# The last recurrent step of a gated graph network computed with nodes on partitions instead of features

## The chip, the cores and the metric

The kernel runs on one core of one Trainium2 chip. The metric is the device time of one execution in microseconds (us). Engines are named as the profile names them: PE is TensorE (matmuls and transposes; PEld is its loading of the stationary operand), DVE is VectorE, ACT is ScalarE, POOL is GpSimd, SP is SyncE, which starts DMAs. [...]

## The reference, cut to what matters

There are 64 graphs of 256 nodes with 256 features each, and two layers. Layer 0 normalizes the nodes' features, takes the positive part and then does three steps of a gated recurrent unit over the graph, whose result is added to x. Layer 1 normalizes again, does graph attention with four heads, and adds that to x.

```
h = relu(layernorm(x))
for i in range(3):                                 # layer 0
    m = h @ weight[i]
    aggr = A^T m                                   # A = (adj != 0)
    r = sigmoid(aggr W_ir^T + b_ir + h W_hr^T + b_hr)
    z = sigmoid(aggr W_iz^T + b_iz + h W_hz^T + b_hz)
    n = tanh(aggr W_in^T + b_in + r * (h W_hn^T + b_hn))
    h = (1 - z) * n + z * h
x = x + h
h = relu(layernorm(x))                             # layer 1
x = x + attention(h, adj, W, b, a)
```

## The kernel before, in words

Two graphs make a pair (PB = 2), so there are 32 pairs of T = 512 nodes. All of the network is done for a pair, and the pairs follow one another in an order that is written out by hand: `at(tick, phase, p, fn)` files a function under a tick, a phase (STEP, then READY, then REST) and a pair, and at the end all are emitted tick by tick, within a phase the later pair first. Nothing reorders them afterwards.

One recurrent step is an object of class `Step`, and it takes six ticks, `tick_0` to `tick_5`. In the steady state three slots of six ticks follow each other: the third step of pair p (slot A in the prediction), the second step of pair p+1 (slot B), the first step of pair p+2 (slot C). In a slot's ticks stands, besides, layer 1 of earlier pairs: its matmuls `po` (L542), its divisions on DVE (L551, L553), its additions to x on POOL (L558), the masks' maxima `any` on DVE (L899), leaky (L919) and exponentials on ACT.

The state is kept transposed in `hT`: features on partitions, two blocks of 128 (KD = 2), nodes in the free dimension. Gates are computed in the same layout. A `block` (L308) is one gate's product for one graph of the pair, or for a sum of both graphs' operands: four fp32 matmuls, the weights stationary (128x128), 256 nodes moving, into one PSUM bank of 512 columns. The products are shared out so that seven instead of eight are needed for a square of products; so there are sums and differences (T1 to T4, T2n, T3n, T4n) on DVE and partial results that are added in PSUM. A `part` (L417) is one matmul of 128x256 of the state's own share of n; there are seven, named N00, N01, NS1 to NS4 and N11.

In `tick_0`, the aggregation (`pa`) multiplies the state with nodes on partitions, split in two halves hNhi and hNlo, with the edges. So at the end of each step the state has to be turned: `back(l, i)` (ticks 7 and 8 of the step, phase REST) does four PE transposes (L770) for each graph into a bank `pback`, and for the first two steps writes hNhi on ACT (L760) and hNlo on DVE (L761). After the third step `residual` (L776) adds the turned state to x on DVE instead.

The steps that the prediction speaks of:

- `tick_1`: NS2 into bank `qb`; DVE's addition (L453) of the first half of `qb` and `m5n` into the second half; the block into `pc`; the part N01.
- `tick_2`: the parts NS3 (it reads T3n, L418) and NS4 into the two halves of `qb`; S1's block. NS3 writes the half that L453 read, and so has to wait for it.
- `state_n` (L421, ACT): the state's share of n is copied out of PSUM with its bias.
- `tanh_half` (L425, ACT): two instructions of 128x256 for R or Z, as each feature block has its own bias per partition.
- `first_n` (L495, DVE): (R+1) * hn into the bank `pn`; `input_n` adds a block onto it; `new_n` (L506 ACT, L510 POOL): two tanhs of 128x256 give n, and POOL subtracts it from the state.
- `update(i)` (L527, L528, DVE): R = (Z+1) * R, then hT = R/2 + n; both graphs' updates stand in phase READY of the tick after `tick_5`, the first tick of the next slot.

PSUM has five banks for gates (`gate_bank`) and three for all else (`bank`). The last pair has a sequence of its own, `plan_tail`, in which layer 1 of the two last pairs is interleaved.

Of the kernel before, what the change touches and what calls it, by code (L numbers as in the profile page):

```python
# [26 lines left out]
def gated_gnn_then_gat_kernel(  # L27
# [69 lines left out]
    def bank(name):  # L97
# [3 lines left out]
        "x": 5, "adj": 2, "edge": 2, "noedge": 2, "hT_a": 2, "xn": 2, "val": 2, "row": 4, "zz": 4, "o": 2,  # L101
# [44 lines left out]
    w_msgs += [load_square("row", f"w_msg_{l}", weight[l]) for l in range(1, L)]  # L146
# [39 lines left out]
    bhn = const.tile([P, KD], F32, name="bhn")  # L186

# [120 lines left out]
    def block(pt, w, j, src, start=False):  # L308

        for c in range(KD):  # L310
            for k in range(KD):
                nc.tensor.matmul(  # L312
                    pt[:, ts(c, N)], w[:, k, j * D + c * P : j * D + (c + 1) * P], src[:, k, :],
                    start=start and c == 0 and k == 0, stop=(c == KD - 1 and k == KD - 1),
                    skip_group_check=True,
                )

# [66 lines left out]
    class Step:  # L384


        def __init__(self, n_, l, hT, end):

            self.n_, self.l, self.hT, self.end = n_, l, hT, end
# [25 lines left out]


# [5 lines left out]

        def tanh_half(self, i, dst, src, g0):
            for c in range(KD):
                nc.scalar.activation(  # L425
                    of(dst, i)[:, c, :], src[:, c, :], AF.Tanh, bias=brz[:, g0 + c : g0 + c + 1], scale=0.5
                )

        def tick_0(self, hN, edge):
            h0 = of(self.hT(), 0)  # L430
            q_a, q_b = self.bank("qa"), self.bank("qb")
            self.part(q_a[:, :N], N00, h0[:, 0, :], start=True)
            nc.scalar.copy(q_b[:, :N], q_a[:, :N])
            aggr = self.own("aggr", [P, KD, T])
            for e in range(KD):
                pt = bank(f"pa_{self.n_}_{e}")
                for i in range(PB):
                    for s in range(KN):
                        for half in range(2):
                            nc.tensor.matmul(  # L440
                                pt[:, ts(i, N)], hN[half][:, i * KN + s, ts(e, P)], edge[:, i * KN + s, :],
                                start=(s == 0 and half == 0), stop=(s == KN - 1 and half == 1),
                            )
                nc.scalar.copy(aggr[:, e, :], pt)
            self.part(q_a[:, N:], NS1, self.T1[:, 0, :])
            nc.scalar.copy(self.own("m5n", [P, N]), q_a[:, N:])  # L446

        def tick_1(self):
            h0 = of(self.hT(), 0)
            q_a, q_b = self.qa, self.qb  # L450
            self.own("hn", [P, KD, T])
            self.part(q_b[:, :N], NS2, self.T2n)
            nc.vector.tensor_add(q_b[:, N:], q_b[:, :N], self.m5n)  # L453
            p_c = self.bank("pc")
            block(p_c, w_h, RH, h0, start=True)
            self.part(q_a[:, :N], N01, h0[:, 1, :])
            self.state_n(0, 0, q_a[:, :N])
            self.bank("p5")
            nc.scalar.copy(self.bank("pd"), p_c)
            T3 = self.own("T3", [P, KD, N])  # L460
            nc.vector.tensor_sub(T3, of(self.aggr, 1), of(self.hT(), 1))
            nc.vector.tensor_add(self.own("T2", [P, KD, N]), T3, h0)

        def tick_2(self):
            q_b = self.qb
            self.part(q_b[:, :N], NS3, self.T3n)
            self.part(q_b[:, N:], NS4, of(self.hT(), 1)[:, 1, :])
            nc.vector.scalar_tensor_tensor(
                of(self.hn, 1)[:, 1, :], q_b[:, :N], bhn[:, 1:2], self.m5n, op0=ALU.add, op1=ALU.add
            )  # L470
            self.state_n(0, 1, q_b[:, N:])
            block(self.p5, w_a[self.l], S1, self.T1, start=True)
            nc.scalar.copy(self.own("m5", [P, T]), self.p5)
            nc.vector.tensor_sub(self.own("T4", [P, KD, N]), self.T2, of(self.aggr, 0))

        def tick_3(self):
            R_ = self.own("R", [P, KD, T])
            block(self.pd, w_a[self.l], S2, self.T2)
            nc.vector.tensor_add(self.bank("pe"), self.pd, self.m5)
            block(self.pc, w_a[self.l], RA, of(self.aggr, 0))  # L480
            self.tanh_half(0, R_, by_c(self.pc), 0)

        def tick_4(self):
            Z_ = self.own("Z", [P, KD, T])
# [3 lines left out]
            block(self.pd, w_h, RZ, self.T3)  # L488
            nc.vector.tensor_add(of(Z_, 1), by_c(self.pd), by_c(self.m5))
            block(self.pe, w_a[self.l], S4, of(self.aggr, 1))  # L490
# [8 lines left out]
        def input_n(self, i):  # L499
            block(getattr(self, f"pn{i}"), w_a[self.l], NA, of(self.aggr, i))  # L500

        def new_n(self, i):
# [6 lines left out]
            if not (self.end and i == 1):  # L509
                nc.gpsimd.tensor_sub(of(self.R, i), of(self.hT(), i), n__)  # L510

        def tick_5(self):
# [3 lines left out]
            block(self.pd, w_a[self.l], ZA, self.T4)  # L516
# [5 lines left out]
        def update(self, i):  # L522

            d_ = of(self.R, i)
            if self.end and i == 1:
                nc.vector.tensor_sub(d_, of(self.hT(), i), of(self.hn, i))
            nc.vector.scalar_tensor_tensor(d_, of(self.Z, i), 1.0, d_, op0=ALU.add, op1=ALU.mult)  # L527
            nc.vector.scalar_tensor_tensor(of(self.hT(), i), d_, 0.5, of(self.hn, i), op0=ALU.mult, op1=ALU.add)  # L528

# [33 lines left out]
    def plan_tail(t0, p, v, g, turn_back, residual):  # L563


        val, zz, own, drow, mrow = None, {}, {}, {}, {}
# [22 lines left out]
        def result(i):  # L589
            if i == 0:  # L590
# [99 lines left out]
        def do(what, q, *key):  # L690
# [3 lines left out]
        order = (  # L694
            lambda: g.update(0), do("rows", 1), do("product", 2, 0), lambda: turn_back(0), lambda: g.update(1),
            do("product", 2, 1), lambda: residual(0), lambda: stats(0), do("add", 1), lambda: turn_back(1),
            do("product", 2, 2), lambda: residual(1), lambda: result(0), lambda: turned(0), lambda: stats(1),
            do("product", 2, 3), do("divided", 2, 0), lambda: values(0), lambda: result(1), lambda: turned(1),
            do("divided", 2, 1), do("divided", 2, 2), lambda: values_out(0), do("divided", 2, 3),
            do("write", 2), lambda: spread_scores(0), lambda: logits(0), lambda: leaky(0),  # L700
            lambda: values(1), lambda: values_out(1), lambda: maxima(0), do("exps", 1, 0), lambda: spread_scores(1),
            lambda: logits(1), lambda: leaky(1), lambda: spread_tops(0), do("product", 1, 0), do("product", 1, 1),
            lambda: maxima(1), lambda: spread_tops(1), do("exps", 1, 1), do("divided", 1, 0), do("divided", 1, 1),
            lambda: exps(0), do("product", 1, 2), do("product", 1, 3), lambda: exps(1), do("divided", 1, 2),
            do("divided", 1, 3), do("write", 1), lambda: output(0), lambda: output(1),
        )
        for k, fn in enumerate(order):
            at(t0 + SUB * (2 * L - 1) + 0.01 * (k + 1), READY, p, fn)

    def plan_pair(p):  # L710
# [40 lines left out]
        def back(l, i):  # L751

            def fn():
                if l < L - 1 and i == 0:
                    v["hN"] = node_halves(f"{p}_{l}")
                turn_back(l, i)
                pt = v["pback", i]
                hi, lo = (flat(y[:, i * KN : (i + 1) * KN, :]) for y in v["hN"])
                if l < L - 1:
                    nc.scalar.copy(hi, pt)  # L760
                    nc.vector.tensor_sub(lo, pt, hi)  # L761
                else:
                    residual(i)
            return fn

        def turn_back(l, i):
            pt = v["pback", i] = bank(f"pback_{p}_{l}_{i}")
            for s in range(KN):
                for k in range(KD):
                    nc.tensor.transpose(  # L770
                        pt[:, s * D + k * P : s * D + (k + 1) * P], h["hT"][:, k, ts(i * KN + s, P)], ident
                    )

        def residual(i):
            xi = flat(v["x"][:, i * KN : (i + 1) * KN, :])
            nc.vector.tensor_add(xi, v["pback", i], xi)  # L776

        for l in range(L):
            end = last and l == L - 1
            g = Step(f"{p}_{l}", l, lambda: h["hT"], end)  # L780
            t = 2 * SUB * l
            ready(t - 3 if l else t - 1, g.state_sums)
            ready(t + 2, g.last_state_sum)
            step(t, lambda g=g: g.tick_0(v["hN"], v["edge"]))
            for k, fn in enumerate((g.tick_1, g.tick_2, g.tick_3, g.tick_4, g.tick_5), 1):
                step(t + k, fn)
            if not end:
                ready(t + SUB, lambda g=g: g.update(0))
                ready(t + SUB, lambda g=g: g.update(1))
                for i in range(PB):  # L790
# [16 lines left out]
        if last:  # L807
            plan_tail(t0, p, v, g, lambda i: turn_back(L - 1, i), residual)
# [169 lines left out]
    at(2, REST, 0, load_vectors)  # L978
    at(5, REST, 0, lambda: step_weights_T(1))
# [38 lines left out]
```

## Time and profile before

| | |
|---|---|
| Median of 3 runs | 2533.7 us (2533.55 to 2534.89) |
| Profiled execution, its own time | 2540.86 us |
| Its span in the profile | 2539.1 us, mean PE clock 0.995 |
| PE busy | 2514.5 us, 99% of the span |
| DVE busy | 1824.1 us, 72% |
| ACT busy | 1466.2 us, 58% |
| POOL busy | 645.5 us, 25% |
| PE transposes of the state (L770) | 768, busy 116.1 us |

The profile shows one execution; its durations are read from it, and the median is what times are compared with. Busy times of matmuls overlap, as they are pipelined, so a PE operation is priced by the distance from its start to the start of the next. An "idle" figure in a row is the time that the engine stood still just before it, and the name behind the arrow is what it waited for.

### The profile page before, as it was taken

How to read it: one execution, taken by the hardware profiler on the slowest of the kernel's cores; microseconds unless marked ns; L12 is line 12 of the kernel's file. 1: busy time of each engine (PE TensorE's matmuls, PEld its weight loads, DVE VectorE, ACT ScalarE, POOL GpSimd, SP SyncE). 2: the span in 40 equal slices, each digit the busy share in tenths (PEclk: the TensorE clock that was granted, in tenths of full speed). 3: DMA queues.
4: the chain of work that ended last, by engine and by line, in shares of the span. 5: the costliest groups of instructions: out<-in, count | busy, mean ns of one | idle time of the engine just before them, and what ended most of it. 6: DMA issues, size and time to landing. Idle time of an engine off the chain costs nothing.

```text
span 2539.1 us, 38539 instructions
## 1 busy us (share of the span) xinstructions
PE 2514.5 (99%) x13918; PEld 2246.4 (88%) x13918; DVE 1824.1 (72%) x4458; ACT 1466.2 (58%) x3095; POOL 645.5 (25%) x514
## 2 busy tenths in 40 slices
PE   8999999999999999999999999999999999999998
PEld 6888898888889888989888988888988889898887
DVE  5567777677777777776777776777777777767667
ACT  3456565565555565555665655655656656556664
POOL 0122232222222222323232323222222223222221
PEclk9999999999999999999999999999999999999998
DMA  3033434553435544345544444534344544354443
GB/s 94 17 74 88 97 93 108 109 125 92 92 92 117 109 113 99 87 95 117 117 100 93 98 102 109 125 92 100 88 113 109 119 95 93 87 124 110 93 95 89
DMA packets 168223, 251.91 MB, mean 99 GB/s; under 512 B 42896, under 2 KB 128352, under 8 KB 168032
## 3 DMA queue, kind: packets, MB, share of 16 engines
q0 software_dynamic: 33728, 130.03, 26.6%
q1 hardware_dynamic: 132736, 119.41, 16.0%
q8 instruction: 110, 1.80, 0.3%
q14 instruction: 81, 0.66, 0.1%
q10 hardware_dynamic: 1568, 0.01, 0.0%
HBM read 215.62 MB, written 25.67 MB: 95 GB/s over the span
## 4 chain that ended last, share of the span: by engine, by line
PE 97%; DVE 1%; DMA 1%; ACT 1%; issue 0%; POOL 0%; SPq 0%; DVEq 0%
PE pd L312 20%; PE pn L312 13%; PE pc L312 13%; PE po L542 9%; PE pa L440 7%; PE qb L418 6%; PE pe L312 6%; PE p L312 6%; PE qa L418 5%; PE pv L820 4%; PE pback L770 3%; PE pt_a L370 1%; PE pt_b L370 1%; PE pc L238 1%; DVE any L899 0%; DMA hh_nat<-in_L_gnn_w_hh_dram 0%
## 5 line engine op out<-in xcount | busy, mean ns | idle before, releaser
L510 POOL TENSOR_TENSOR R<-hT_a,hn 128x512 f32<-128x512 f32 x191 | 317.8, 1664 | 879.4 <-ACT hn L506 821.5
L312 PE MATMUL pn<-aggr,w_a 128*128 128x256 f32 x1536 | 367.1, 382 | 0.0
L312 PE MATMUL pd<-T,w_a 128*128 128x256 f32 x1536 | 366.3, 381 | 0.0
L312 PEld LDWEIGHTS pn<-aggr,w_a 128*128 128x128 f32 x1536 | 287.0, 190 | 43.1 <-DVE pn L495 6.4
L312 PEld LDWEIGHTS pd<-T,w_a 128*128 128x128 f32 x1536 | 287.9, 191 | 37.6
L542 PEld LDWEIGHTS po<-val,zz 128*128 128x128 f32 x2048 | 250.3, 195 | 4.5
L542 PE MATMUL po<-val,zz 128*128 128x65 f32 x2048 | 247.2, 275 | 0.0
L899 DVE CUSTOM_DVE_ANT_0 any<-drow,noedge 128x256 f32<-128x256 f32 x496 | 236.9, 478 | 9.8 <-DMA drow<-score_dram 1.0
L506 ACT ACTIVATE hn<-pn,bi 128x256 f32<-128x256 f32 x384 | 160.3, 469 | 144.3 <-PE pn L312 144.2
L425 ACT ACTIVATE R<-pc,brz 128x256 f32<-128x256 f32 x192 | 80.5, 470 | 278.5 <-PE pc L312 278.5
L527 DVE SCALAR_TENSOR_TENSOR R<-Z,R 128x512 f32<-128x512 f32 x192 | 131.8, 687 | 147.6 <-POOL R L510 142.8
L558 POOL TENSOR_TENSOR x<-x,o 128x256 f32<-128x256 f32 x124 | 112.0, 904 | 481.6 <-DVE o L553 481.6
L761 DVE TENSOR_TENSOR hNlo<-pback,hNhi 128x512 fp32r<-128x512 f32 x128 | 88.4, 691 | 201.6 <-ACT hNhi L760 201.6
L919 ACT ACTIVATE zz<-zz,val 128x256 f32<-128x256 f32 x496 | 224.9, 509 | 0.0
L495 DVE SCALAR_TENSOR_TENSOR pn<-R,hn 128x512 f32<-128x512 f32 x192 | 142.5, 742 | 93.7 <-ACT hn L421 77.2
L425 ACT ACTIVATE R<-pe,brz 128x256 f32<-128x256 f32 x192 | 80.5, 470 | 185.9 <-PE pe L312 185.9
L528 DVE SCALAR_TENSOR_TENSOR hT_a<-R,hn 128x512 f32<-128x512 f32 x192 | 174.6, 909 | 14.3 <-ACT m5n L446 1.4
L312 PE MATMUL pd<-T,w_h 128*128 128x256 f32 x768 | 181.5, 379 | 0.0
L312 PE MATMUL pc<-aggr,w_a 128*128 128x256 f32 x768 | 181.5, 379 | 0.0
L312 PE MATMUL pe<-aggr,w_a 128*128 128x256 f32 x768 | 181.4, 379 | 0.0
L312 PE MATMUL pc<-hT_a,w_h 128*128 128x256 f32 x768 | 181.4, 379 | 0.0
L312 PE MATMUL p<-T,w_a 128*128 128x256 f32 x768 | 181.4, 379 | 0.0
(176 smaller groups left out, 5258.5 us busy)
## 6 DMA issues: line engine op xcount, KB each, us to landing
zz<-score_dram POOLq DMA_DIRECT2D x62, 1024.0 KB, 11.7
zz<-topT_dram POOLq DMA_DIRECT2D x62, 1024.0 KB, 8.7
adj<-in_adj_dram SPq DMA_DIRECT2D x64, 512.0 KB
drow<-score_dram SPq DMA_DIRECT2D x62, 512.0 KB
x<-in_x_dram SPq DMA_DIRECT2D x32, 512.0 KB
out_dram<-x SPq DMA_DIRECT2D x31, 512.0 KB
noedge_dram<-noedge SPq DMA_DIRECT2D x31, 256.0 KB
score_dram<-score SPq DMA_DIRECT2D x124, 4.0 KB
```

Of the source, the lines that this page charges most:

```text
L312: nc.tensor.matmul(pt[:, ts(c, N)], w[:, k, j * D + c * P : j * D + (c + 1) * P], src[:, k, :], start=start and c == 0 and k == 0, stop=(c ...
L418: nc.tensor.matmul(pt, w_n[:, j, :], src, start=start, stop=True, skip_group_check=True)
L425: nc.scalar.activation(of(dst, i)[:, c, :], src[:, c, :], AF.Tanh, bias=brz[:, g0 + c : g0 + c + 1], scale=0.5)
L440: nc.tensor.matmul(pt[:, ts(i, N)], hN[half][:, i * KN + s, ts(e, P)], edge[:, i * KN + s, :], start=(s == 0 and half == 0), stop=(s == KN ...
L495: nc.vector.scalar_tensor_tensor(by_c(self.bank(f"pn{i}")), of(self.R, i), 1.0, of(self.hn, i), op0=ALU.add, op1=ALU.mult)
L506: nc.scalar.activation(n__[:, c, :], p_n[:, c, :], AF.Tanh, bias=bi[:, 2 * KD + c : 2 * KD + c + 1])
L510: nc.gpsimd.tensor_sub(of(self.R, i), of(self.hT(), i), n__)
L527: nc.vector.scalar_tensor_tensor(d_, of(self.Z, i), 1.0, d_, op0=ALU.add, op1=ALU.mult)
L528: nc.vector.scalar_tensor_tensor(of(self.hT(), i), d_, 0.5, of(self.hn, i), op0=ALU.mult, op1=ALU.add)
L542: nc.tensor.matmul(po[:, ts(h_, VC)], zz[:, j, h_, ts(s, P)], v["val"][:, i * KN + j, ts(h_, VC)], start=(j == 0), stop=(j == KN - 1),)
L899: nc.vector.tensor_tensor_reduce(any_, drow[r // KN][:, h, :], v["noedge"][:, r, :], 1.0, -3.0e38, ALU.add, ALU.max, accum_out=v["top"][:, ...
L919: nc.scalar.activation(zz[:, h, :], zz[:, h, :], AF.Prelu, alpha=ALPHA, bias=v["val"][:, r, S0 + H + h : S0 + H + h + 1],)
```

## The change

The third step of layer 0 gets a class of its own, `LastStep`, in which nodes are on partitions and features in the free dimension. Its `block` has the state stationary and the weights moving, with as many matmuls of the same size; each `part` becomes two matmuls of 128x128. The result comes out as x is stored, so the third step has no `back` and no `residual`; its update adds to x directly, in three DVE operations for each graph: x += n, R = (Z+1) * R, x += R/2. For that, the state before the step is needed with nodes on partitions in full precision: `back` of the second step copies it to a buffer `h` on ACT.

Biases now run along the free dimension, so they can't be given to ACT as one value per partition. Four rows, broadcast to all partitions (`b_rows`), are loaded with six DMAs at tick 3 and combined by four DVE operations at tick 9. R's bias is put into the bank `pc` by an ACT copy at tick 0 (`seed`), n's into both `pn` banks by ACT copies in tick 4; Z's is added by DVE in tick 4, and that of the state's share of n by DVE in `state_n` and `last_state_n`. `state_n` of this step moves from ACT to DVE. The tanhs become one instruction of 512 in place of two of 256. `first_n` writes to SBUF, and `new_n` adds it to the bank on DVE before the tanh.

The order changes too. In tick 5, `pn0` and `pn1` come before ZA's block; `new_n(1)` and Z's tanh of graph 0 move to phase REST of tick 5; the update moves from phase READY of the next tick to its phase REST. In the tail graph 1 comes first. The buffers tagged `row` go from 4 to 2, and two of the weights are loaded into buffers tagged `noedge`. Here is the diff's core.

```diff
-        "x": 5, "adj": 2, "edge": 2, "noedge": 2, "hT_a": 2, "xn": 2, "val": 2, "row": 4, "zz": 4, "o": 2,
+        "x": 5, "adj": 2, "edge": 2, "noedge": 2, "hT_a": 2, "xn": 2, "val": 2, "row": 2, "zz": 4, "o": 2,
...
+    class LastStep(Step):
+        both = [P, PB, KN * D]
+        def mine(self, y, i):
+            return by_c(y[:, i, :])
+        def block(self, pt, w, j, src, start=False):
+            for s in range(KN):
+                for k in range(KD):
+                    nc.tensor.matmul(
+                        pt[:, ts(s, D)], src[:, k, ts(s, P)], w[:, k, ts(j, D)],
+                        start=start and s == 0 and k == 0, stop=(s == KN - 1 and k == KD - 1),
+                        skip_group_check=True,
+                    )
+        def part(self, pt, j, src, start=False):
+            for s in range(KN):
+                nc.tensor.matmul(
+                    pt[:, ts(s, P)], src[:, ts(s, P)], w_n[:, j, :], start=start and s == 0, stop=True,
+                    skip_group_check=True,
+                )
...
+        def state_n(self, c, i, pt):
+            nc.vector.tensor_add(
+                self.mine(self.hn, i)[:, :, ts(c, P)], pt.rearrange("q (s n) -> q s n", s=KN), self.row(BH, c)
+            )
+        def tanh_half(self, i, dst, src, g0):
+            nc.scalar.activation(self.mine(dst, i), src, AF.Tanh, scale=0.5)
+        def first_term(self):
+            return self.pc, False
+        def seed(self):
+            nc.scalar.copy(by_c(self.bank("pc")), self.row(BR))
+        def first_n(self, i):
+            hn_ = self.mine(self.hn, i)
+            nc.vector.scalar_tensor_tensor(hn_, self.mine(self.R, i), 1.0, hn_, op0=ALU.add, op1=ALU.mult)
+        def new_n(self, i, h):
+            hn_ = self.mine(self.hn, i)
+            p_n = by_c(getattr(self, f"pn{i}"))
+            nc.vector.tensor_add(p_n, p_n, hn_)
+            nc.scalar.activation(hn_, p_n, AF.Tanh)
+            if not (self.end and i == 1):
+                nc.gpsimd.tensor_sub(self.mine(self.R, i), self.nodes(h, i), hn_)
+        def tick_4(self):
...
+            for i in range(PB):
+                nc.scalar.copy(by_c(self.bank(f"pn{i}")), self.row(BI))
+            self.block(self.pd, w_h, RZ, self.T3)
+            nc.vector.tensor_add(by_c(self.pd), by_c(self.pd), self.row(BZ))
+            nc.vector.tensor_add(self.mine(Z_, 1), by_c(self.pd), by_c(self.m5))
...
+        def tick_5(self, h):
+            self.first_n(1)
+            self.input_n(0)
+            self.input_n(1)
+            self.tanh_half(1, self.Z, self.mine(self.Z, 1), KD)
+            self.block(self.pd, w_a[self.l], ZA, self.T4)
+            self.new_n(0, h)
+        def tick_5_rest(self, h):
+            self.new_n(1, h)
+            self.tanh_half(0, self.Z, by_c(self.pd), KD)
+        def update(self, i, h, x_):
+            d_, n__, xi = self.mine(self.R, i), self.mine(self.hn, i), self.nodes(x_, i)
+            if self.end and i == 1:
+                nc.vector.tensor_sub(d_, self.nodes(h, i), n__)
+            nc.vector.tensor_add(xi, xi, n__)
+            nc.vector.scalar_tensor_tensor(d_, self.mine(self.Z, i), 1.0, d_, op0=ALU.add, op1=ALU.mult)
+            nc.vector.scalar_tensor_tensor(xi, d_, 0.5, xi, op0=ALU.mult, op1=ALU.add)
...
-                turn_back(l, i)
-                pt = v["pback", i]
...
-                if l < L - 1:
-                    nc.scalar.copy(hi, pt)
-                    nc.vector.tensor_sub(lo, pt, hi)
-                else:
-                    residual(i)
+                nc.scalar.copy(hi, pt)
+                nc.vector.tensor_sub(lo, pt, hi)
+                if l == L - 2:
+                    nc.scalar.copy(flat(v["h"][:, i * KN : (i + 1) * KN, :]), pt)
...
-            if not end:
-                ready(t + SUB, lambda g=g: g.update(0))
-                ready(t + SUB, lambda g=g: g.update(1))
-                for i in range(PB):
+            if final:
+                step(t + 5, lambda g=g: g.tick_5(v["h"]))
+                rest(t + 5, lambda g=g: g.tick_5_rest(v["h"]))
+            else:
+                step(t + 5, g.tick_5)
+            for i in range(PB):
+                if final and not last:
+                    rest(t + SUB, lambda g=g, i=i: g.update(i, v["h"], v["x"]))
+                elif not final:
+                    ready(t + SUB, lambda g=g, i=i: g.update(i))
                     rest(t + SUB + 1 + i, back(l, i))
```

## The prediction

> **What bounds the kernel now.** I read the busy shares first, then the chain of waits, then stretches of the steady state, and last one slot's timeline.
>
> ```profile
> PE 2514.5 (99%) x13918; PEld 2246.4 (88%) x13918; DVE 1824.1 (72%) x4458; ACT 1466.2 (58%) x3095; POOL 645.5 (25%) x514
> PE 97%; DVE 1%; DMA 1%; ACT 1%; issue 0%; POOL 0%; SPq 0%; DVEq 0%
> 1000.00:1400.00 400.00, 400.00 (x2215) 358.12 (x2214) 291.35 (x713) 235.48 (x496) 104.43 (x81) 1.00 0.46 105
> ```
>
> The last line is 400 us of the middle: PE busy 400.00, DVE 291.35, ACT 235.48, POOL 104.43, PE clock 1.00. PE never waits, so a pair (76.95 us) costs the sum of its PE work, and PE work removed is worth its full length unless another engine then comes late. DVE's 73% leaves room on average only. The place that matters is slot B, the second step of pair p+1, into which pair p's update of its third step falls. DVE there, around 1354 us, then PE and POOL:
>
> ```profile
> 1353.87 0.18 DVE L551 RECIPROCAL rden<-po 128x4 f32<-128x4 f32 x1 [2.20 <-PE po L542]
> 1354.16 0.42 DVE L553 TENSOR_TENSOR o<-po,rden 128x256 f32<-128x256 f32 x1
> 1354.50 0.68 DVE L527 SCALAR_TENSOR_TENSOR R<-Z,R 128x512 f32<-128x512 f32 x1
> 1355.22 1.12 DVE L528 SCALAR_TENSOR_TENSOR hT_a<-R,hn 128x512 f32<-128x512 f32 x1
> 1356.26 0.68 DVE L527 SCALAR_TENSOR_TENSOR R<-Z,R 128x512 f32<-128x512 f32 x1
> 1357.04 0.69 DVE L528 SCALAR_TENSOR_TENSOR hT_a<-R,hn 128x512 f32<-128x512 f32 x1
> 1357.65 0.42 DVE L899 CUSTOM_DVE_ANT_0 any<-drow,noedge 128x256 f32<-128x256 f32 x1
> ...
> 1358.46 0.43 DVE L453 TENSOR_TENSOR qb<-qb,m5n 128x256 f32<-128x256 f32 x1
> ```
>
> ```profile
> 1358.66 0.59 PE L418 MATMUL qa<-hT_a,w_n 128*128 128x256 f32 x2
> 1359.09 0.60 PE L770 MATMUL pback<-ident,hT_a 128*128 128x128 f32 x4
> 1359.53 0.60 PE L418 MATMUL qb<-T3n,w_n 128*128 128x256 f32 x2
> ```
>
> ```profile
> 1349.66 1.72 POOL L510 TENSOR_TENSOR R<-hT_a,hn 128x512 f32<-128x512 f32 x1 [0.86 <-ACT hn L506]
> 1353.06 1.27 POOL L510 TENSOR_TENSOR R<-hT_a,hn 128x512 f32<-128x512 f32 x1 [1.68 <-ACT hn L506]
> 1354.66 1.12 POOL L558 TENSOR_TENSOR x<-x,o 128x256 f32<-128x256 f32 x1 [0.34 <-DVE o L553]
> ```
>
> From L551, where DVE picks up a product of PE, to the end of L453, DVE is without a gap. The matmul NS3 (qb<-T3n, tick 2) writes what L453 read and waits for it: L453 ends at 1358.89, NS3 starts at 1359.53. This slack of 0.64 us comes back in the same place in the other pairs; the smallest I found where PE did not wait is 0.28. In slots A and C the same slack is 1.60 and 3.37.
>
> [...] an `any` at 1350.30 beside POOL's R took 1.37 us for its usual 0.42, and L528 above took 1.12 beside L558 for its median 0.69. [...] the trace has 0.109 us per 128-wide fp32 record, and transposes go at that pitch. [...] rows here have 681 to 693, at a pitch of 0.60 when independent of the one before and 0.72 when dependent.
>
> **The change part by part.** Per pair, in us.
>
> PE. (a) The third step no longer turns its state back: 8 transposes x 0.109 = −0.87 (the group of four above takes 1359.53−1359.09 = 0.44). For 31 pairs before the tail −27.0; nothing hides them, as PE is full. (b) A `block` has the same eight fp32 matmuls of 128x256 with the operands exchanged: 0. A `part` was one matmul of 128x256 at a pitch of 0.432 and becomes two of 128x128, four records x 0.109 to 0.112 = 0.436 to 0.448; seven parts: +0.03 to +0.11, I take +0.06, x32 = +2.
>
> ACT. Four tanhs of 512 (pitch about 0.58) for eight of 256 (0.84 a pair), three state_n go to DVE; added are the seed of pc, two seeds of pn and two copies of h. The sum is within 0.5 us of nothing, on an engine busy 59%. What matters is when. Seed of pc: I place it at about 1327.9 in slot A against the first block on pc at 1328.2, margin 0.3; nothing, cover thin. Seeds of pn: ready 4 us before pn0. Copies of h: behind hNlo, about 1.4 us before PE wants the `bank` again. All taken as nothing.
>
> DVE. Removed: one update of 4 operations, two residual additions (2 x 0.6), two first_n into PSUM become two into SBUF. Added: update of 6, three state_n (3 x 0.34), one more in the last state_n, Z's bias (0.6), two pn+=hn (2 x 0.6). In all +3.7 per pair, about +120 busy us. Slots A and C have room: T2 by 1332.6 for pd's block at 1335.8; pe's sum at 1338.8 for 1341.5; Z(1) at 1344.8 for 1350.2. These cost nothing; without that cover each would cost its own 0.3 to 0.6.
>
> Slot B has none. The update moves from READY to the end of tick 0, and everything in it precedes L453. From L551's start, by pitches: rden 0.29, o 0.34, two `any` 0.92, then twice x+=n 0.60, R 0.72, x+=R/2 0.61: 5.41. Before it was 1358.46−1353.87 = 4.59 (0.38 of it contention). So L453 starts at 1353.87+5.41 = 1359.28 and ends at 1359.71, plus a contention C. PE without the transposes is at NS3 at 1359.53−0.44 = 1359.09, while it could start only at 1359.71+0.28+C = 1359.99+C. **A stall of 0.90+C appears where 0.87 was saved.** Behind NS3 stand NS4 and S1's block, that is all of PE; DVE's state sum and ACT's m5 wait for them. No transposed state is needed in between.
>
> C is not in the trace; from both sides. Nothing, if no DVE operation meets POOL: C = 0. If only the x+=o of POOL meets an update, as L528 does now: 0.38. What I take: pn0's addition follows PE's pn0 at 1348.6, the four xn_a and two `any` follow, POOL's R(0) meets the latter and holds one for 0.96 (as at 1350.30), so pn1's addition is at about 1352.6, tanh n1 by 1354.0, and POOL's R(1) stands at 1354.05 to 1355.3, across the two `any` in front of the update: 0.74, then x+=o across x+=n: 0.43. C = 1.17. Top: both POOL operations held against the updates in full, 1.7. C below 0 would need DVE to start sooner against PE; L551 waits for PE's po, and no removed transpose stands on PE between the two, so I exclude it.
>
> Queues. SP: six more DMAs at tick 3 of the start, of 128 KB each, behind other loads; four DVE operations at tick 9: nothing. POOL: the same subtractions, the last pair apart. Buffers `row` 4 to 2 and w_msg in `noedge`: start only, nothing.
>
> Tail (last pair): transposes −0.87, two residuals gone, but DVE has state_n 0.34, Z's bias 0.6 and two pn additions 1.2 on the way to the last scores; PE's one wait there is 1.5 us for `top`, and its clock drops to 0.50 at 2486.9 for 17.1 us. I take +1 with ±4 for the clock.
>
> **Sum.** −27.0 (transposes, 31 pairs) + 2 (parts) + 30 x (0.90+1.17) = +62.1 (I leave one slot of the 31 without a stall, as the start is loose) + 1 = **+38**. The profiled execution took 2540.86 with a span of 2539.1, 0.28% above the median of 2533.7; against its own time the sum gives 2579, against the median 2572.
>
> **Rivals.** Within 0.2% means within 5 us, about what a measurement can tell here.
>
> 1. *The gain arrives.* L453 is not late: DVE's order lets its queue be 0.9+C shorter than I count, because the operations overlap more than their pitch or the update's dependent ones run at 0.60. Then −27+2+1: about 2510. For: DVE idles 2.20 us before L551, so it is not loaded in that stretch. Against: that gap is ahead of L551, which waits for PE; after it there is none. It decides if L453 ends by 1358.81, 0.90 earlier than I have it. 11%.
> 2. *Break-even.* C between 0 and 0.1: the stall takes exactly the saving, −27+2+27 to 30+1 = +3 to +6: 2537 to 2540; with 0.38, +15: 2548. For: POOL is busy only 25% of the time, so the update may fall where it rests. Against: 1.12 for 0.69 is in the trace. 20%.
> 3. *C of 1.2* as worked: 2572. 54%.
> 4. *More than one stall.* C = 1.7, or the pc seed is late by 0.5 beyond its margin of 0.3 in every slot A as ACT's copy is queued behind tick 0's aggr copy: 30 x 0.5 more, 2587 to 2600. 15%.
> 5. *It doesn't do what it says*: a bank held longer delays the order. The banks' numbers are unchanged and `bank` has three with one user less, so I put it within 4.
>
> **How the numbers follow.** Likeliest: case 3, 2572. The range takes break-even's lower end with the tail's −4 below it, 2530, to case 4 at 2600; it leaves out the gain (11%) and a little above. Faster by over 0.2%: case 1, 0.11. Within: the low part of case 2, 0.08. Slower: 0.81.
>
> **What would show it.** In the changed profile: PE busy per 400 us about 393 to 388 in the steady state, with waits of PE's qb (T3n) for DVE's qb sum as the largest, 30 times about 2 us; DVE busy near 1945; PE's pback row x512; `any` or updates of 1.0 us and more beside POOL's R. If PE stays at 400.00 and the period falls to 76.1, case 1 holds; if the largest wait names pc or pn, case 4.

## The result, and the profile after

The changed kernel takes 2560.6 us (median of 4 runs, 2560.04 to 2562.97) against 2534.1 for the kernel before on the same chip: 1.0106 times as long, with an interval of 1.0089 to 1.0124. That is +26.5 us. Faster was given 0.11, slower 0.81; the forecast was 2572, in a range of 2530 to 2600. The profiled execution took 2561.0 us with a span of 2559.0. The one of before was among the longer runs of its kernel, so two profiled spans differ by only 19.9 us; the section on the tail comes back to this.

The first view is the page's busy times and the chain that ended last, and the busy times in the same 400 us of the steady state (PE, PEld, DVE, ACT, POOL, then PE's clock, the DMA share and GB/s).

```profile
PE 2494.6 (97%) x14110; PEld 2230.7 (87%) x14110; DVE 1931.8 (75%) x4686; ACT 1462.4 (57%) x2967; POOL 627.7 (25%) x514
PE 88%; DVE 8%; issue 2%; ACT 1%; DMA 0%; DVEq 0%; POOL 0%; SPq 0%
1000.00:1400.00 400.00, 393.90 (x2242) 353.47 (x2241) 305.24 (x734) 236.09 (x481) 104.93 (x84) 1.00 0.46 105
```

PE has less to do (2494.6 for 2514.5) and is no longer always busy: 393.90 of 400. DVE now holds 8% of the chain where it held 1%, though it is busy only three quarters of the time. The list of PE's waits (us in total, times, longest) names one place:

```profile
PE qb L446 <- DVE qb L494: 36.7, 31, 1.4
```

All the others on the list come once or twice. This is slot B: NS3 waits for the addition into qb, in 31 of the 32 pairs (before, it waited for it in none). DVE's, PE's and POOL's timeline there (start, duration):

```profile
1287.52 0.18 DVE L686 RECIPROCAL rden<-po 128x4 f32<-128x4 f32 x1 [0.83 <-PE po L677]
1287.81 0.42 DVE L688 TENSOR_TENSOR o<-po,rden 128x256 f32<-128x256 f32 x1
1288.15 0.81 DVE L1036 CUSTOM_DVE_ANT_0 any<-drow,noedge 128x256 f32<-128x256 f32 x1
...
1289.00 0.84 DVE L1036 CUSTOM_DVE_ANT_0 any<-drow,noedge 128x256 f32<-128x256 f32 x1
...
1289.78 0.68 DVE L661 TENSOR_TENSOR x<-x,hn 128x512 f32<-128x512 f32 x1
...
1293.02 0.69 DVE L663 SCALAR_TENSOR_TENSOR x<-R,x 128x512 f32<-128x512 f32 x1
1293.63 0.42 DVE L494 TENSOR_TENSOR qb<-qb,m5n 128x256 f32<-128x256 f32 x1
```

```profile
1292.30 0.59 PE L446 MATMUL qa<-hT_a,w_n 128*128 128x256 f32 x2
1294.11 0.70 PE L446 MATMUL qb<-T3n,w_n 128*128 128x256 f32 x2 [1.22 <-DVE qb L494]
1294.65 0.59 PE L446 MATMUL qb<-hT_a,w_n 128*128 128x256 f32 x2
```

```profile
1287.40 1.28 POOL L626 TENSOR_TENSOR R<-h,hn 128x512 f32<-128x512 f32 x1 [2.28 <-ACT hn L624]
1288.64 0.92 POOL L693 TENSOR_TENSOR x<-x,o 128x256 f32<-128x256 f32 x1
```

From the start of rden to that of L494 it is 6.11 us, where it was 4.59. PE finishes N01, stands still, and starts NS3 0.06 us after L494 has ended. The first matmul after the wait takes 0.54 to the next start in place of 0.43. Two maxima take 0.81 and 0.84 us instead of 0.42, each beside a POOL operation; `o` beside the same POOL operation keeps its 0.42; it reads a PSUM bank, and the maxima read two SBUF tiles.

Measured between the same matmuls of each pair, in medians over the steady state:

| us | before | after |
|---|---|---|
| a pair | 76.95 | 77.63 |
| slot A's stretch | 28.497 | 28.566 |
| slot B's stretch | 23.297 | 23.903 |
| slot C's stretch | 25.153 | 25.164 |
| slot B, NS2 to NS3 | 3.027 | 3.972 |

With four transposes less and nothing to wait for, NS3 would follow NS2 by 3.027 − 0.435 = 2.59 us. So PE loses 1.38 us there in each pair; the list's 1.2 counts only from the modelled end of the matmul before.

### The profile page after: what moved, and what is told of

Same layout as the page of the kernel before. It is cut to its first block, busy times and chain, and to the rows that moved or that the text cites. A ratio compares the mean times of both kernels' runs of the same rounds, so it can differ in the third digit from the quotient of the medians.

```text
span 2559.0 us, 39091 instructions
## 1 busy us (share of the span) xinstructions
PE 2494.6 (97%) x14110; PEld 2230.7 (87%) x14110; DVE 1931.8 (75%) x4686; ACT 1462.4 (57%) x2967; POOL 627.7 (25%) x514
## 3 DMA queue, kind: packets, MB, share of 16 engines
q0 software_dynamic: 33728, 130.03, 26.5%
## 4 chain that ended last, share of the span: by engine, by line
PE 88%; DVE 8%; issue 2%; ACT 1%; DMA 0%; DVEq 0%; POOL 0%; SPq 0%
PE pd L437 13%; PE pn L437 9%; PE po L677 8%; PE pc L437 6%; PE pd L578 6%; PE pa L481 5%; PE pe L437 4%; PE p L437 4%; PE pv L957 4%; PE pc L578 4%; PE qb L446 4%; PE pn L578 4%; PE qb L586 2%; PE p L578 2%; PE pback L896 2%; PE pe L578 2%
## 5 line engine op out<-in xcount | busy, mean ns | idle before, releaser
L548 POOL TENSOR_TENSOR R<-hT_a,hn 128x512 f32<-128x512 f32 x128 | 224.1, 1750 | 772.3 <-ACT hn L545 714.4
L437 PE MATMUL pn<-aggr,w_a 128*128 128x256 f32 x1024 | 244.3, 381 | 0.0
L437 PE MATMUL pd<-T,w_a 128*128 128x256 f32 x1024 | 243.6, 381 | 0.0
L437 PEld LDWEIGHTS pn<-aggr,w_a 128*128 128x128 f32 x1024 | 192.1, 190 | 31.1 <-DVE pn L534 6.1
L437 PEld LDWEIGHTS pd<-T,w_a 128*128 128x128 f32 x1024 | 193.0, 191 | 26.0
L481 PE MATMUL pa<-edge,hNhi 128*128 128x256 f32 x512 | 133.6, 299 | 0.0
L1009 ACT ACTIVATE zz<-link 128x1024 f32<-128x1024 bf16 x124 | 130.7, 1056 | 3.4 <-DMA link<-noedge_dram 3.4
L1071 ACT ACTIVATE zz<-zz 128x1024 f32<-128x1024 f32 x124 | 131.8, 1065 | 0.0
L485 ACT COPY aggr<-pa 128x512 f32<-128x512 f32 x192 | 107.1, 596 | 34.6 <-PE pa L481 34.6
L481 PE MATMUL pa<-edge,hNlo 128*128 128x256 f32 x512 | 125.2, 282 | 1.3 <-DVE hNlo L901 1.3
```

The costliest lines, as they stand in the source:

```text
L437: nc.tensor.matmul(pt[:, ts(c, N)], w[:, k, j * D + c * P : j * D + (c + 1) * P], src[:, k, :], start=start and c == 0 and k == 0, stop=(c ...
L481: nc.tensor.matmul(pt[:, ts(i, N)], hN[half][:, i * KN + s, ts(e, P)], edge[:, i * KN + s, :], start=(s == 0 and half == 0), stop=(s == KN ...
L1009: nc.scalar.activation(logits[i][:, j, :, :], v["link"][:, j : j + 1, ts(i, N)].to_broadcast([P, H, N]), AF.Identity, scale=1 / 16,)
L1071: nc.scalar.activation(zz, zz, AF.Exp)
```

## The experiments

The theory is that only the length of DVE's queue between rden and L494 decides, and that POOL's two operations are part of that length ("queue theory"). Its rival is that DVE has too much work in the whole slot, so that a wait only changes its place ("load rival"). DVE ran its operations in the order of the code where an edit moved them: behind the addition stand four maxima instead of two in any_later (from 1285.23, the addition at 1283.57), and the update of graph 1 in split (from 1272.76, the addition at 1272.42).

**One pair of maxima moved behind L494.**

```diff
-            ready(43 + y if not late else 45 + (3 * y) // 8, maxima(r, h0))
+            ready((49 if y == 5 else 43 + y) if not late else 45 + (3 * y) // 8, maxima(r, h0))
```

> The changed kernel with one pair of mask maxima (any, 0.92 us of DVE by pitch, 1.63 as they ran beside POOL) moved from the tick of the update to the next one, behind the addition into qb (L494). Queue theory (NS3 waits only because L494 stands at the end of DVE's queue): the queue is shorter by 1.63 us, more than the stall of 1.38, so PE qb<-DVE qb goes from 31 waits to nearly none, PE is busy all the time again, and the period falls from 77.63 to 76.95 - 0.87 + 0.07 = 76.15 us; time about 2560.6 - 31 x 1.48 = 2515. Load rival (DVE has too much to do in the whole slot, so the wait only moves to the next DVE result): another wait of PE of about 1.4 us appears for L452, T or pd, and the time stays at 2550 to 2561.

It took 2541.7 us, 1.0024 times the kernel before (1.0017 to 1.0032), and 76.95 a pair. Both expectations failed: the gain is 19 us, not 46, but what is left is the old wait, not another one. The timeline of this kernel shows why:

```profile
1278.14 0.18 DVE L686 RECIPROCAL rden<-po 128x4 f32<-128x4 f32 x1 [0.83 <-PE po L677]
1278.43 0.42 DVE L688 TENSOR_TENSOR o<-po,rden 128x256 f32<-128x256 f32 x1
1278.77 1.08 DVE L661 TENSOR_TENSOR x<-x,hn 128x512 f32<-128x512 f32 x1
1279.77 1.23 DVE L662 SCALAR_TENSOR_TENSOR R<-Z,R 128x512 f32<-128x512 f32 x1
1281.03 0.69 DVE L663 SCALAR_TENSOR_TENSOR x<-R,x 128x512 f32<-128x512 f32 x1
```

POOL's two operations (1278.02 for 1.28, 1279.26 for 1.19) now hold the update, 1.08 for 0.68 and 1.23 for 0.68, instead of the maxima. I had counted the maxima's delay as going with them. The queue is 5.43 long, 0.68 shorter than 6.11, and the wait 0.68 shorter.

**The same with the transposes put back.**

```diff
+                    rest(t + SUB + 1 + i, turn_again(i))   # four transposes of hT into a bank, not read
```

> The kernel any_later with the eight transposes per pair of the state after the third step put back on PE (into a bank that nobody reads). Queue theory: PE is full there, so they cost their full 8 x 0.109 = 0.87 us: 31 x 0.87 = 27 us above any_later, about 2542, period 77.02. Load rival: PE has room, so they cost less than half of that.

2554.0 us, +12.3, half of what the queue theory gave, because the wait at NS3 was still there. The pair takes 77.39, +0.44: the first four transposes hide in that wait (NS2 to NS3 stays at 3.29), the others cost their full 0.435. By the letter of the expectation, less than half of 27 is the load rival's figure; but the room that PE had was the old wait, and no other one appeared.

**The changed kernel with the transposes put back.**

> The changed kernel with the same eight transposes per pair put back, nothing read from them. Queue theory: the first four stand between N01 and NS3, where PE stands still anyway for L494, and cost nothing; the other four come behind NS3 and cost 0.44: 31 x 0.44 = +13.5, about 2574, and the wait PE qb<-DVE qb falls by 0.44 us each to about 0.8. Load rival or a PE bound everywhere: +27, 2588, with the waits unchanged.

2576.6 us, against 2574 expected, a pair 78.07 (+0.44). NS2 to NS3 stays at 3.971, and the wait shrinks from 36.7 in all to

```profile
PE qb L446 <- DVE qb L494: 23.2, 30, 1.0
```

So half of the transposes that the change removed were worth nothing, as DVE sets the time there.

**POOL's subtraction of graph 1 left out.**

```diff
-            if not (self.end and i == 1):
+            if i == 0:
                 nc.gpsimd.tensor_sub(self.mine(self.R, i), self.nodes(h, i), hn_)
```

> The changed kernel without POOL's subtraction h - n of graph 1 in the third step (its update then works on R itself). Queue theory with POOL holding DVE: of the two maxima ahead of the update, that ran 0.81 and 0.84 us beside POOL's R and x+=o, one is free again (0.42) and the other still meets x+=o: the queue is 0.4 us shorter, 31 x 0.4 = 12 us less, about 2548. If POOL does not hold DVE (the maxima are slow for another cause): no change, 2560; if x+=o alone were the cause, no change either.

2549.1 us, against 2548 expected. The queue is 5.71, 0.40 shorter, and the pair 77.23, 0.40 shorter: the first of the two maxima takes 0.42, the second still 0.84 beside x+=o.

**Neither of the two POOL operations.**

> The changed kernel with neither of the two POOL operations that run beside the end of the update's queue: the subtraction h - n of graph 1 in the third step, and the addition of o to x for the last of a pair's four node blocks (both left out of the result). It measures the bare queue. Queue theory with POOL holding DVE: both maxima take 0.42 again, from rden to L494 5.4 us in place of 6.11, the wait of NS3 is 0.7 shorter than in the changed kernel (1.38) and about 0.7 remains, period 77.63-0.7 = 76.93, just that of the kernel before: 2560.6 - 31 x 0.7 = 2539. If POOL's hold on DVE were worth less than no_r1 showed in full (0.4), period above 77.1; if the queue without POOL were no longer than before, 76.15 and 2515.

2537.4 us, 1.0007 (0.9997 to 1.0016) of the kernel before, against 2539 expected; 76.82 a pair against 76.93.

```profile
1277.87 0.41 DVE L1037 CUSTOM_DVE_ANT_0 any<-drow,noedge 128x256 f32<-128x256 f32 x1
...
1278.33 0.42 DVE L1037 CUSTOM_DVE_ANT_0 any<-drow,noedge 128x256 f32<-128x256 f32 x1
...
1282.54 0.42 DVE L494 TENSOR_TENSOR qb<-qb,m5n 128x256 f32<-128x256 f32 x1
```

Rden starts at 1277.24, so the bare queue is 5.30 us. POOL's hold on DVE is the rest of the 6.11 to 6.12, C = 0.82 us a pair. Without it the change comes out about even: of the 0.80 us a pair that PE's own work became shorter (76.95 to 76.15), the bare queue alone eats 0.67.

**The update of graph 1 moved behind L494.**

```diff
+            for fn in waiting.pop(self.n_, ()):      # in tick_1, right after the addition into qb
+                fn()
...
-                    rest(t + SUB, lambda g=g, i=i: g.update(i, v["h"], v["x"]))    # for i == 1
+                    waiting[f"{p + 1}_{L - 2}"] = [lambda g=g, i=i: g.update(i, v["h"], v["x"])]
```

> The changed kernel with the update of graph 1 (x+=n, R, x+=R/2) moved behind the addition L494 on DVE; nothing else. Queue theory: from the start of rden (L686) L494 ends after 0.29+0.34+0.92+1.93+0.43 = 3.91 plus 0.7 to 0.95 of contention with POOL = 4.6 to 4.9 us, and PE could start NS3 at 5.21; so there is no wait any more, the period is 76.95-0.87+0.07 = 76.15, PE is busy 400 of 400 us, and the time is 2560.6 - 31 x 1.48 = about 2515, faster than the kernel before. Load rival (DVE has too much in the slot, as moving the maxima did not bring the gain): T2 (L503), which is now 1.9 us later in the queue, comes late for S2's block (pd), and PE waits there instead; 2535 to 2560.

2517.2 us, 0.9932 (0.9918 to 0.9947) of the kernel before; a second series gave 2517.5. A pair takes 76.15, as expected, and the wait is gone from the list. The steady state, then L495, which is L494 in this kernel, and NS3:

```profile
1000.00:1400.00 400.00, 400.00 (x2282) 360.67 (x2281) 308.14 (x750) 240.12 (x485) 105.76 (x85) 1.00 0.46 106
```

```profile
1272.42 0.42 DVE L495 TENSOR_TENSOR qb<-qb,m5n 128x256 f32<-128x256 f32 x1
```

```profile
1273.45 0.59 PE L448 MATMUL qb<-T3n,w_n 128*128 128x256 f32 x2
```

PE is full again, with all of the change's operations still there and DVE at 308.14, more than before. What cost the time was where one half of the update stood.

**Both: the update of graph 1 and the maxima behind L494.**

> The kernel split with the pair of maxima moved behind L494 as in any_later too. Queue theory: L494 had room already, so the same as split within 3 us, about 2515. Load rival: T2 comes 0.9 us sooner than in split, so this one is faster than split by up to 31 x 0.9 = 28 us if split waits for T2.

2525.8 us, 76.39 a pair: slower than the last one by 8.5, which neither theory gave. L494 now has 1.29 us to spare, but the maxima stand ahead of the addition pe = pd + m5 (L522), which ends late for RZ's block into pd. This pair has the longest such delay of the steady state, 0.39 us; in the median of the pairs the block comes 0.22 us late, about the 0.24 that a pair became longer:

```profile
1281.65 0.69 DVE L522 TENSOR_TENSOR pe<-pd,m 128x512 f32<-128x512 f32 x1
```

```profile
1282.40 2.00 PE L439 MATMUL pd<-T,w_h 128*128 128x256 f32 x8 [0.23 <-DVE pe L522]
```

The update stands elsewhere, but this is the load rival's mechanism: the next wait is close. In the kernel before this one L522 ended at 1280.71 for a block that started at 1280.80, so there is hardly any room left in DVE's order.

**The kernel before with its update in phase REST.**

```diff
-                ready(t + SUB, lambda g=g: g.update(0))
-                ready(t + SUB, lambda g=g: g.update(1))
+                when = rest if l == L - 1 else ready
+                when(t + SUB, lambda g=g: g.update(0))
+                when(t + SUB, lambda g=g: g.update(1))
```

> The kernel before with one edit: the update of the third step (two operations each) in phase REST of its tick instead of READY, as the change places it. Queue theory: L453 stays behind the same operations (the two maxima and the update change places), 4.6 us from rden, and has 0.64 us to spare; no change, 2534 within 5. Rival (it is the update's place that costs, not the operations that it gained): slower by 10 us or more.

2535.1 us, 1.0008 (0.9999 to 1.0017); 76.95 a pair. The later phase alone, with the update's old operations, costs nothing that can be measured. So the cost lies in the longer update at that place, with the contention that it meets.

**The changed kernel without R's bias.**

```diff
         def first_term(self):
-            return self.pc, False
+            return self.bank("pc"), True
         def seed(self):
-            nc.scalar.copy(by_c(self.bank("pc")), self.row(BR))
+            pass
```

> The changed kernel without R's bias: no ACT copy into pc at tick 0 of the third step, the first block clears the bank. It leaves b_r out. Queue theory: that copy is off the path, slot A does not wait for it; 2560 within 3, the period stays 77.63. Rival (the seed holds up ACT's copies of qb and aggr and with them PE, or keeps a gate bank that another needs): slot A gets shorter, 0.1 us a pair or more.

2561.2 us, 77.64 a pair, slot A 28.575. R's bias at the beginning of the step is free.

**PE kept busy in the tail.** From the first NS2 matmul of the last step to the end, the changed kernel took 72.7 us in its profile. The kernel before took 74.8 in one profile and its version with the moved update 68.0. These are windows of 10 us, 24 to 35 us into that stretch, of before, of before with the moved update, and of the changed kernel (PE's clock is the third number from the right):

```profile
2488.00:2498.00 10.00, 10.00 (x50) 10.00 (x48) 7.42 (x23) 3.56 (x9) 4.55 (x5) 0.50 0.43 86
```

```profile
2490.00:2500.00 10.00, 9.03 (x68) 8.08 (x68) 8.22 (x27) 2.91 (x7) 6.73 (x8) 1.00 0.54 101
```

```profile
2511.00:2521.00 10.00, 8.02 (x47) 7.48 (x47) 8.80 (x26) 2.52 (x6) 5.80 (x7) 0.68 0.50 87
```

The clock halves there in some executions. In the changed kernel the clock falls during the second of two waits of PE:

```profile
PE ptopT L974 <- DVE top L1047: 2.2, 1, 2.2
PE pt_b L741 <- DVE xn_b L732: 2.0, 1, 2.0
```

In the kernel before the first was 1.5, and the second 0.5 or absent. So I filled both with work that leads to nothing:

```diff
+            if i == u:                               # and the same ahead of the transposes of topT
+                for _ in range(14):
+                    nc.tensor.transpose(pt[:, :P], ident, ident)
```

> The kernel split with 14 transposes of the identity, 1.5 us of PE, put into each of the two stretches of the last pair in which PE waits for DVE (2.18 us ahead of ptopT, 1.96 ahead of the first pt_b); their result is overwritten. Clock theory (these waits let the PE clock fall to 0.50, for 10 us from 28 us after the last step's N-sum on, and that is the 4 us that the tail costs more than in the kernel before): the clock stays at 1.00 there, and the time is 3 to 5 us below split, 2513. If the drop has another cause, the clock drops as before and the time is the same as split's or up to 3 us longer.

> The kernel split once more, on the same chip as split_warm: 2517 within 2 us.

2513.0 us (2512.76 to 2513.5) with the 28 transposes, 2517.5 (2514.27 to 2519.47) without. The ratios to the kernel before are 0.9907 (0.9894 to 0.9919) and 0.9924 (0.9910 to 0.9938), so the two intervals overlap, but the runs themselves do not. Windows of 10 us, 28 us into the stretch, with the transposes and without:

```profile
2470.00:2480.00 10.00, 9.15 (x69) 8.11 (x68) 8.61 (x24) 1.91 (x4) 6.76 (x8) 1.00 0.78 133
```

```profile
2470.00:2480.00 10.00, 8.30 (x48) 7.43 (x49) 7.84 (x22) 1.19 (x2) 6.37 (x8) 0.83 0.70 136
```

More work on PE made the kernel faster by 4.5 us and its runs alike. This is the fastest version here.

## Why the prediction was right, and which terms were off

The mechanism was right: NS3's wait takes the place of the transposes removed, in slot B, 31 times. The sum came out at +38, the measurement at +26.5. The stalls were taken for too much, 30 x 2.07 = 62.1 us where 31 x 1.48 = 45.9 were measured; the tail and the start, taken for too little, gave back 4 to 5 of these 16, which is luck. By its terms:

- **Transposes, −0.87 a pair.** Right. Where PE is full (the kernel split), the pair is 76.15 = 76.95 − 0.87 + 0.07.
- **Parts, +0.06.** Slot A shows 28.566 − 28.497 = +0.07.
- **The stall without contention, 0.90.** Too large. By no_pool's queue, L494 would end at 5.30+0.42 after rden, and NS3 could follow 0.055 later, 5.775. PE could have been there at 5.66−0.435 = 5.225 (1359.53 less 1353.87 in before, less a group of transposes). That is 0.55. Two terms were mis-sized: the step from L494's end to NS3, taken as 0.28 because that was the smallest gap seen where PE did not wait, is 0.06 where it does; and the two maxima, counted at 0.92 a pair, take 0.81 from the start of the first to the start of the next operation, as before's own lines show (1357.65 to 1358.46), which is the difference between 5.41 and 5.30. The six operations of the update, rows of 128x512 with 0.68 or 0.69 each, take the 3.86 that were counted (1289.78 to 1293.63).
- **Contention, C = 1.17.** Too large; it is 0.82. The walk had POOL's R(0) hold the maxima ahead of pn1's addition and so delay R(1). It held the fourth xn_a instead (1.36 for 0.41), and pn1's addition was early enough. R(1) began 0.12 ahead of rden, not 0.18 after it, so R(1) and x+=o met one of the two maxima each (0.39 and 0.42 over) and nothing of the update. The 0.38 that the prediction reads as contention in before's queue is 0.43 by its lines (L528 takes 1.04 to the next start, the second time 0.61); only a rival's 2548 rests on it.
- **What was not in the sum.** The first matmul after the wait costs 0.11 more. With 0.55+0.82 = 1.37 and 0.11, a pair is −0.87+0.07+1.37+0.11 = +0.68, which is 77.63−76.95.
- **ACT and the queues: nothing.** Right as far as tried: no_seed changed nothing, and no wait of PE for the seeds or the h copies recurs with the pairs. One `pwv` at the start waits 1.6 us for the copy of h, once.
- **Start and tail, +1 within ±4.** The last step's NS2 stands 22.0 us later in the profile: 19.0 in 28 pairs of 0.68, 1.9 in the first three and 1.1 between the last two steps. The other 4.5 of the medians' 26.5 are the tail's. Its bare work is about what was forecast: without a drop of the clock the stretch takes 69.3 us in split_warm and 68.0 in before_moved, and the rest of the 4.5 is the clock's, within the ±4. Why the two waits are longer than before is not shown: PE has fewer transposes there, DVE has more operations, and the order of the tail is another.

The measured 2560.6 lies halfway between break-even's upper figure, 2548, and the forecast. Break-even's case of C near 0 is no_pool, and its time came out (2537.4, for 2537 to 2540), but by luck: the bare stall is 0.55 and not 0.90, so that 0.13 us a pair of the saving is left, and the start and the tail use that up. The rival that the gain arrives is refuted for this order, and split shows how little was lacking: L494 has to end 1.38 us sooner.

## What to carry to other kernels

On an engine that is full on average, price an operation removed at its length only up to the point where the next producer is late; price that producer's whole queue from its last wait, with the pauses that a neighbour engine imposes as entries of the queue. Two operations of 0.6 us more in front of one addition, 0.4 us more of contention there and a tail 4.5 us longer turned a saving of 27 us into a loss of 26, while the same operations with half of the update behind it gave a kernel 0.7% faster than the one before. Moving an operation out of a contended stretch need not take the contention with it: in any_later it went to what stood there next (1.08 and 1.23 us for 0.68).

## What the runs showed of the hardware that was not expected

In the stretch in front of L494, POOL's operations on two SBUF tiles held DVE's for 0.39 to 0.55 us when these read two SBUF tiles (0.81 and 0.84 for 0.42; 1.08 and 1.23 for 0.68), and for 0.95 in the case of xn_a (at 1283.91 in the changed kernel, 1.36 for 0.41), which reads one tile. `o`, which reads PSUM, was not held: 0.42 at 1287.81, beside POOL's R. What decides which operations are held, no run here shows.

The hold is no fixed toll. Measured by its end, a held operation of 512 columns ended 0.55 us after POOL's operation, a held maximum of 256 columns 0.28 after it, and xn_a 0.15. These three figures are medians over the steady state, and they are the same in before, where an `any` was held for 0.96, as in the changed kernel, where it was held for 0.4. So these holds were 0.13 to 0.26 us shorter than what POOL's operation still had to run when DVE's began: the ends above less the bare 0.68, 0.42 and 0.41. Where DVE's operation began first, POOL's was the longer one: hn<-R,hn, begun at 1281.18, kept its 0.68 us, and the first of these two took 1.10 where it took 0.72 at 1271.74; the second is the one that held xn_a:

```profile
1281.34 1.10 POOL L693 TENSOR_TENSOR x<-x,o 128x256 f32<-128x256 f32 x1 [5.03 <-DVE o L688]
1283.80 1.31 POOL L626 TENSOR_TENSOR R<-h,hn 128x512 f32<-128x512 f32 x1 [1.36 <-ACT hn L624]
```

PE's clock fell at different distances from its waits in the tail. In the changed kernel and in split it fell during the second of two waits of 2.2 and 2.0 us with 5.6 us of PE work between them: in the changed kernel that wait lasts from 2513.72 to 2515.68, and the clock is 1.00 up to 2514.24 and 0.59 in the 2 us from there. In no_pool it fell behind the first wait alone, of 2.2: it was 1.00 in the 4 us that hold the wait (2481.90 to 2485.90), 0.52 in the next 4 and 0.50 in the 12 after those. In the profile of before it fell at 2486.9, 1.7 us after a single wait of 1.5, and stayed at 0.50 for 17.1 us. With the two waits filled, in split_warm, it was 1.00 in that stretch. What decides when it falls, the runs do not show. The drop also differs between executions of one kernel: the kernel before ran mostly near 2534 but sometimes at 2540 to 2543, its mean PE clock then mostly 0.994 to 0.996 instead of 0.998 or 0.999.
